# State loop of a two-layer network: whole uses of a PSUM bank, a piece cut in three, copies that alternate between two buffers, pieces handed out later

## Chip, cores and metric

One core of a Trainium2 chip runs the whole program as one launch. The metric is the device time of that launch in microseconds, median of several runs. The core's engines run their own instruction queues in order and wait for one another through semaphores: TensorE (PE in the profile, its weight loads PEld), VectorE (DVE), ScalarE (ACT), GpSimd (POOL) and SyncE (SP, which here only starts DMA transfers).

## The reference, cut to what matters

Two transformer-like layers on 64 sequences of 64 tokens with 256 features, all in float32. The first layer has a conditioned scan, an attention with 16 heads and a quantized feed-forward net. In the second, a recurrent net feeds a selective state-space block, and then come a mixture of experts with a shared expert and a second mixture. The change is in the state-space block and in the shared expert:

```python
xz = x @ W_in                       # 256 -> 2 x 512: xi and the gate z
xc = silu(causal_conv(xi) + b_conv) # four taps
delta_lr, B, C = split(xc @ W_xproj, [16, 32])
delta = softplus(delta_lr @ W_dt + b_dt)
dA  = exp(delta[..., None] * A)     # 512 channels x 16 states
dBx = delta[..., None] * B[:, :, None, :] * xc[..., None]
h   = dA_t * h + dBx_t              # along the 64 tokens
y   = sum_n(h * C_t) + D * x_t
out = (y * silu(z)) @ W_out

h = silu(x @ s_w1.T) * (x @ s_w3.T) # the shared expert, two of them side by side
shared = h @ s_w2.T
```

## The kernel before

Features lie on the 128 partitions and tokens along the free axis. Tokens are cut into eight chunks of 512 (eight whole sequences each). The function `mamba` runs the state-space block as one loop of 256 steps, 32 for each chunk. A step `j` of a chunk treats one state `n` (16 of them) of one pair of channel blocks `p` (two pairs of two blocks of 128). The first half of a chunk's steps has pair 0, the second half pair 1.

What one step does:

- `inputs` (L1046, two steps ahead, on POOL): hb = dx times the row of B, over 128 x 1024. The row of B is spread over the partitions by a DMA (Bn, L993, on SP), two states per transfer, in two buffers. hb has five buffers.
- `decay` (L1053, one step ahead, on ScalarE): dA = exp(delta * A), two activations of 128 x 504, into three PSUM banks that are used in turn.
- two scans (L1094, VectorE): h = dA * h + hb, each over 512 tokens.
- one product (L1096, VectorE): hb times cb. cb is the row of C spread over the partitions by a matmul (L998) into the one PSUM bank `cb`, one step ahead; the next such matmul waits until the product has read the bank.
- eight transposing matmuls (L1109, TensorE) that sum the products of a half's 16 states in the two banks `yp0` and `yp1`.

Everything else is handed out in pieces beside the steps. `turn` takes one piece at a time out of two streams:

- `urgent`: `finish` (L1006, L1008, L1009: transposing the sums back, adding D * xc, multiplying with the gate), after each half; and after a chunk's last step `project` (L1023, L1026: the output projection in two blocks of 256/2 rows, four matmuls each, added to x; a load of x, L1016, and a store, L1028, on SP).
- `pieces`: `gates` (L982, L985, L988: the matmuls of z, copies, SiLU) for a pair, and `head` of the next chunk: four blocks of convolution (L919 matmuls, L923 on ScalarE, three taps L926 on VectorE each), a SiLU (L930), the projection to delta, B and C (L934 to L947, with the store of B by L940), and for each pair delta and dx (L958 matmuls, L959 to L964 and L969 on ScalarE, then L967, L970, L971, L972 on POOL, or on VectorE for chunk 0).

A generator that yields `MID` is half-way through a use of the bank `mp`, the one bank that all pieces share. `turn` goes on with `pieces` after any `MID`, also one that came out of `urgent` (only `project` yields such a one). In each chunk 40 turns are spread evenly over the 32 steps: that is the number of pieces of a chunk. A loop in front of `inputs` takes extra turns if the delta and dx of a step that comes up aren't made.

A third stream, `others`, is the work of the mixture for the chunk before (`Mixture.beside`): its routing scores (L1499, L1505, L1511), from chunk 5 on the sending of rows (`send`: a load of `xr`, L1794, transposes L1802, copies L1803, eight indirect DMAs L1343 on POOL), and the shared expert (`shared`): matmuls L1820, four for each copy, into the one bank `mq`, copies L1824 (first factor) and L1827 (second factor, into the tile `up`, which POOL multiplies in by L1828), one SiLU L1831, matmuls L1836 and the scaled copy L1840 into `up`, stored by L1842. All these tiles have one buffer each.

The program is written with a layer that builds the dependencies and orders each engine's instructions at build time, by their place in the program and by its own cost estimates; the two scans and the product of the steps keep their written order. So a piece that is handed out elsewhere may move other instructions too.

ScalarE holds one set of function tables at a time. Exp, Ln and SiLU are in different sets here; the profile shows each change as ACT_TABLE_LOAD.

After the loop, `mixtures` runs the experts' tiles, with the shared expert of the last chunk and the sending of three further chunks between its first tiles.

Of the kernel before, what the change touches and what calls it, by code (L numbers as in the profile page):

```python
# [13 lines left out]
F32 = mybir.dt.float32  # L14
# [7 lines left out]
P = 128  # L22
B, L, D = 64, 64, 256
NT = B * L
CH = 512
NCH = NT // CH
KD = D // P
# [830 lines left out]
MID, END = "mid", "end"  # L858


def mamba(g, w, hs, beside):
# [3 lines left out]
    nc, tc = g.nc, g.tc  # L865
    NI, S, R = w.NI, w.S, w.R
# [3 lines left out]
    NB = 2  # L870
    PI = 2
    STEPS = NI // PI * S
    LEFT = 40
    BESIDE = 56
    BESIDE_LAST = 72
    hs2 = hs.rearrange("p k b t -> p k (b t)")
# [1 line left out]
    with (  # L878
# [17 lines left out]
        rows = 2 * 32 + S  # L896
# [12 lines left out]
        def head(c, v):  # L909

            tok = ts(c, CH)
            v.xc = p2.tile([P, NI, CH], F32, name="xc")
            v.delta, v.dx, v.sz, v.ready = [], [], [], 0
            v.dbc = p1.tile([W, CH], F32, name="dbc")
            v.parts = parts[c % 2]
            for i in range(NI):
                ps = one()
                for k in range(KD):
                    nc.tensor.matmul(ps, w.Win[:, k, ts(i, P)], hs2[:, k, tok], start=(k == 0), stop=(k == KD - 1))  # L919
                    if k == 0:  # L920
                        yield MID
                acc = v.xc[:, i, :]
                nc.scalar.activation(acc, ps, AF.Identity, bias=w.col[:, 0, i : i + 1], scale=w.taps[:, i, 3:4])  # L923
                for s in range(1, 4):
                    to = seq(acc)[:, :, s:]
                    nc.vector.scalar_tensor_tensor(  # L926
                        to, seq(ps)[:, :, : L - s], w.taps[:, i, 3 - s : 4 - s], to, ALU.mult, ALU.add
                    )
                yield
            nc.scalar.activation(v.xc, v.xc, AF.Silu)  # L930
            yield
            ps = one()
            for i in range(NI):
                nc.tensor.matmul(ps[:W, :], w.Wxp[:, i, :], v.xc[:, i, :], start=(i == 0), stop=(i == NI - 1))  # L934
                if i < NI - 1:
                    yield MID
            nc.scalar.copy(v.dbc, ps[:W, :])

            v.B = tc.dram_tile((S, CH), F32, name=f"B{c}")
            nc.sync.dma_start(v.B, v.dbc[R : R + S, :])  # L940


            r = slice(C0, W)
            nc.scalar.copy(v.parts[32 : 32 + S, :], ps[r, :])
            nc.vector.tensor_sub(ps[r, :], ps[r, :], v.parts[32 : 32 + S, :])
            nc.scalar.copy(v.parts[0:S, :], ps[r, :])
            nc.vector.tensor_sub(v.parts[64 : 64 + S, :], ps[r, :], v.parts[0:S, :])  # L947
            yield


            for i0 in range(0, NI, PI):
                z, u = (p3.tile([P, PI, CH], F32, name=n) for n in ("delta", "dx"))
                v.delta.append(z)
                v.dx.append(u)
                t2, t3 = (p1.tile([P, PI, CH], F32, name=n) for n in ("t2", "t3"))
                for i in range(PI):
                    ps = one()
                    nc.tensor.matmul(ps, w.Wdt[:, ts(i0 + i, P)], v.dbc[:R, :], start=True, stop=True)  # L958
                    nc.scalar.activation(z[:, i, :], ps, AF.Relu, bias=w.col[:, 1, i0 + i : i0 + i + 1])  # L959
                    nc.scalar.activation(u[:, i, :], ps, AF.Abs, bias=w.col[:, 1, i0 + i : i0 + i + 1])  # L960
                    yield
                nc.scalar.activation(u, u, AF.Exp, scale=-1.0)
                nc.scalar.activation(t2, u, AF.Identity, bias=unit[:, 0:1])
                nc.scalar.activation(t3, t2, AF.Identity, bias=unit[:, 1:2])  # L964
                yield
                e = nc.gpsimd if c else nc.vector
                e.tensor_sub(u, t3, u)  # L967
                yield
                nc.scalar.activation(t2, t2, AF.Ln)  # L969
                e.tensor_add(z, z, t2)  # L970
                e.tensor_sub(z, z, u)  # L971
                e.tensor_mul(u, z, v.xc[:, i0 : i0 + PI, :])  # L972
                v.ready += PI
                yield
# [94 lines left out]
        urgent, pieces, others = iter(()), iter(()), iter(())  # L1069
        mid = None  # L1070

        def turn():

            nonlocal mid
            got = next(pieces, None) if mid else next(urgent, END)
            if got is END:
                got = next(pieces, None)
            mid = got

        for s in range(LAST):  # L1080
            c, j = divmod(s, STEPS)
            p, n = divmod(j, S)
            now = vs[c]
            if j == 0:
                ahead = head(c + 1, vs[c + 1]) if c + 1 < NCH else iter(())
                pieces = chain(pieces, gates(c, now, 0), islice(ahead, 3 * NI + PI + 4), gates(c, now, PI), ahead)
                left = 0
            if n == 0:
                yp = [pp.tile([P, CH // P, P], F32, name=f"yp{i}") for i in range(PI)]
            hb, dA = hbs.pop(s), decays.pop(s)  # L1090

            for i in range(PI):
                h = hb[:, i, :]
                ins = nc.vector.tensor_tensor_scan(h, dA[i].rearrange("p b l -> p (b l)"), h, 0.0, ALU.mult, ALU.add)  # L1094
                tc.stamp_issue_order_token(ins.ins, "state")
            ins = nc.vector.tensor_tensor(hb, hb, cb.unsqueeze(1).to_broadcast([P, PI, CH]), ALU.mult)  # L1096
            tc.stamp_issue_order_token(ins.ins, "state")
            if s + AHEAD < LAST:
                ca, ja = divmod(s + AHEAD, STEPS)
                while vs[ca].ready <= ja // S * PI:  # L1100
                    turn()
                inputs(s + AHEAD)
            if s + 1 < LAST:
                decay(s + 1)
                cb = spread_c(vs[(s + 1) // STEPS], (s + 1) % S)

            for i in range(PI):
                for t in range(CH // P):
                    nc.tensor.matmul(  # L1109
                        yp[i][:, t, :],  # L1110
                        hb[:, i, ts(t, P)],
                        g.ident,
                        start=(n == 0 and t == 0),
                        stop=(n == S - 1 and t == CH // P - 1),
                        is_transpose=True,
                        skip_group_check=True,
                    )
            if n == S - 1:
                yT = [p1.tile([P, CH // P, P], F32, name=f"yT{i}") for i in range(PI)]
                for i in range(PI):  # L1120
                    nc.scalar.copy(yT[i], yp[i])
                urgent = chain(urgent, finish(c, now, p * PI, yT))
                if j == STEPS - 1:
                    urgent = chain(urgent, project(c, now))
            while left < (j + 1) * LEFT // STEPS:
                left += 1
                turn()
            most = BESIDE if c + 1 < NCH else BESIDE_LAST
            for _ in range((j + 1) * most // STEPS - j * most // STEPS):
                next(others, None)  # L1130
# [578 lines left out]
class Mixture:  # L1709
# [97 lines left out]
    def shared(self, c, x, work):  # L1807

        g, nc = self.g, self.g.nc
        NS = self.s1.shape[2] // P  # L1810
        UT = CH // 2
        for u in range(2):
            xu = x[:, :, ts(u, UT)]
            h = work.tile([P, NS, UT], F32, name="sh")
            for w in (self.s1, self.s3):
                for i in range(NS):
                    if i % 2 == 0:
                        ps = bank(g, (P, 2, UT))
                    for k in range(KD):
                        nc.tensor.matmul(ps[:, i % 2, :], w[:, k, ts(i, P)], xu[:, k, :], start=(k == 0), stop=(k == KD - 1))  # L1820
                    if i % 2:
                        to = h[:, i - 1 : i + 1, :]
                        if w is self.s1:
                            nc.scalar.copy(to, ps)  # L1824
                        else:
                            up = work.tile([P, 2, UT], F32, name="up")
                            nc.scalar.copy(up, ps)  # L1827
                            nc.gpsimd.tensor_mul(to, to, up)  # L1828
                    yield
                if w is self.s1:  # L1830
                    nc.scalar.activation(h, h, AF.Silu)  # L1831
                    yield
            ps = bank(g, (P, 2, D))
            for t in range(2):
                for i in range(NS):
                    nc.tensor.matmul(ps[:, t, :], h[:, i, ts(t, P)], self.s2[:, i, :], start=(i == 0), stop=(i == NS - 1))  # L1836
                    if i % 2 and (t, i) != (1, NS - 1):
                        yield
            rows = work.tile([P, 2, D], F32, name="up")
            nc.scalar.mul(rows, ps, 0.125)  # L1840
            to = self.made[c * CH + u * UT : c * CH + (u + 1) * UT, :]
            nc.sync.dma_start(to.rearrange("(t p) d -> p t d", p=P), rows)  # L1842
# [346 lines left out]
```

## Time and profile before

| | us |
|---|---|
| median of three runs (2806.24 to 2814.49) | 2806.84 |
| the profiled execution | 2807.03 |
| its span | 2804.6 |
| state loop, from the first scan to the last step | 698.5 to 1846 |
| what follows the loop | 1846 to 2804.6 |
| busy in the whole span: TensorE / VectorE / ScalarE / POOL | 2339.3 / 1770.7 / 1375.5 / 1340.5 |

Length of the eight chunks, from the first scan of one to the first scan of the next, read from the timeline of VectorE:

| chunk | 0 | 1 | 2 | 3 | 4 | 5 | 6 | 7 |
|---|---|---|---|---|---|---|---|---|
| us | 135.5 | 136.9 | 142.6 | 143.0 | 158.0 | 140.9 | 143.3 | 147 |

A line of the costliest groups reads: line, engine, operation, tile written and tiles read, shapes, count, then the group's busy time and the mean of one in ns, and last the engine's idle time ahead of it with what ended most of it. A line of waits reads: who waited, for whom, us in total, how often, and the longest. A timeline line has the start, the length, the engine and the instruction, and in brackets how long the engine had been idle and what ended that.

### The profile page before, as it was taken

To read this page: it belongs to the slowest core of one execution; us is meant where nothing else is said; L and a number is where in the kernel's file an instruction comes from. 1 tells how busy PE (TensorE), PEld (TensorE's weight loads), DVE (VectorE), ACT (ScalarE), POOL (GpSimd) and SP (SyncE) were. 2 spreads that over 40 slices of the span, in tenths; PEclk is the share of its full clock that TensorE was granted. 3 is DMA by queue.
4 is the path that set the end of the run, shared out by engine and by line. 5 is a ranking of instruction groups with operands and counts; after the bars stand their busy time and mean duration, and the time that the engine had idled before them with its cause. 6 is when DMAs were issued, how large, how long until landed. Compare 5 with 4: busy or idle time off the path is not lost.

```text
span 2804.6 us, 34388 instructions
## 1 busy us (share of the span) xinstructions
PE 2339.3 (83%) x11977; PEld 1674.0 (60%) x11996; DVE 1770.7 (63%) x2980; ACT 1375.5 (49%) x2289; POOL 1340.5 (48%) x1166
## 2 busy tenths in 40 slices
PE   3989967996568888887978888687786989999995
PEld 3634436773345555554655555566664768888884
DVE  0477748973999898888889797852353442322333
ACT  0567528885466757584757676533232222222220
POOL 0022345521696868685878787835555331111110
PEclk9979988997769999998999999899998999999997
DMA  9999820002112122221121222325685755555655
GB/s 224 372 358 347 276 70 1 1 1 90 68 68 83 65 74 70 72 72 57 65 92 67 83 81 75 106 70 178 212 287 194 278 216 206 214 192 197 227 192 189
DMA packets 180501, 406.03 MB, mean 145 GB/s; under 512 B 24785, under 2 KB 84434, under 8 KB 174946
## 3 DMA queue, kind: packets, MB, share of 16 engines
q1 hardware_dynamic: 166882, 366.80, 38.4%
q0 software_dynamic: 13440, 36.98, 3.4%
q8 instruction: 96, 1.57, 0.2%
q14 instruction: 83, 0.68, 0.1%
HBM read 280.76 MB, written 144.98 MB: 152 GB/s over the span
## 4 chain that ended last, share of the span: by engine, by line
PE 43%; DVE 21%; ACT 13%; issue 9%; POOL 5%; another core or an unknown queue 2%; DMA 1%; DVEq 0%; SPq 0%; ACTq 0%; POOLq 0%
DVE hb L1094 12%; PE ps L1684 11%; PE acc L1582 8%; PE out L450 4%; DVE hb L1096 3%; ACT dA L1053 2%; PE ps L1651 2%; PE yp L1109 2%; PE mq L1820 1%; DVE xc L926 1%; PE s L416 1%; PE acc L441 1%; ACT L1053 1%; PE mp L982 1%
## 5 line engine op out<-in xcount | busy, mean ns | idle before, releaser
L1046 POOL TENSOR_TENSOR hb<-dx,Bn 128x1024 f32<-128x1024 f32 x256 | 606.4, 2377 | 269.0 <-PE yp L1109 219.7
L1094 DVE TENSOR_TENSOR_SCAN hb<-dA,hb 128x512 f32<-128x512 f32 x512 | 602.1, 1210 | 63.2 <-ACT dA L1053 59.8
L1053 ACT ACTIVATE dA<-delta,negA 128x504 f32<-128x504 f32 x512 | 345.6, 685 | 303.5 <-DVE hb L1094 298.3
L1109 PEld LDWEIGHTS yp<-ident,hb 128*128 128x128 f32 x2048 | 264.4, 150 | 160.2 <-issue 121.2
L1096 DVE TENSOR_TENSOR hb<-hb,cb 128x1024 f32<-128x1024 f32 x256 | 312.4, 1220 | 66.3 <-PE cb L998 48.0
L1684 PE MATMUL ps<-gxT,w 128*128 128x256 f32 (+1 forms) x1600 | 324.5, 361 | 1.2 <-DVE gxT L1559 0.8
L1684 PEld LDWEIGHTS ps<-gxT,w 128*128 128x128 f32 x1600 | 276.3, 190 | 47.2 <-issue 12.4
L1820 PE MATMUL mq<-x,moe_s 128*128 128x256 f32 x896 | 244.5, 405 | 66.1 <-ACT up L1827 29.9
L1109 PE MATMUL yp<-ident,hb 128*128 128x128 f32 x2048 | 298.6, 290 | 0.0
L1358 POOL DMA_INDIRECT ffn_y<-gy,to x72 | 69.2, 962 | 432.3 <-ACT gy L1584 419.8
L1820 PEld LDWEIGHTS mq<-x,moe_s 128*128 128x128 f32 x896 | 166.6, 200 | 131.7 <-ACT sh L1824 42.5
L1688 DVE TENSOR_TENSOR gh<-gs,ps 128x256 f32<-128x256 f32 (+1 forms) x200 | 78.6, 394 | 213.5 <-ACT gs L1687 206.2
L1582 PE MATMUL acc<-w,gh 128*128 128x256 f32 (+1 forms) x864 | 190.0, 390 | 0.0
L1584 ACT ACTIVATE gy<-acc,wt 128x256 f32<-128x256 f32 x152 | 67.4, 474 | 246.8 <-PE acc L1582 227.5
L1687 ACT ACTIVATE gs<-ps 128x256 f32<-128x256 f32 (+1 forms) x200 | 72.4, 364 | 235.4 <-PE ps L1684 219.3
L998 PE MATMUL cb<-parts,pick 80*128 80x512 bf16 x256 | 104.5, 408 | 88.2 <-DVE hb L1096 83.9
L1582 PEld LDWEIGHTS acc<-w,gh 128*128 128x128 f32 (+1 forms) x864 | 146.8, 191 | 30.4 <-issue 13.2
L432 POOL TENSOR_TENSOR E<-E,z 128x1024 f32<-128x1024 f32 x32 | 61.6, 1925 | 194.5 <-DVE z L431 118.0
L1358 POOL DMA_INDIRECT moe_y<-gy,to x80 | 78.0, 975 | 110.2 <-ACT gy L1584 91.3
L1582 PE MATMUL acc<-w,rh 128*128 128x256 f32 x320 | 88.5, 419 | 45.6 <-ACT rh L1653 40.3
L1572 DVE TENSOR_REDUCE wt<-pick 128x2 f32<-128x4 f32 (+1 forms) x88 | 13.6, 156 | 174.7 <-ACT gy L1584 164.0
L450 PE MATMUL out<-oT,hs 128*128 128x512 f32 x256 | 117.8, 604 | 1.5 <-ACT oT L443 1.5
(470 smaller groups left out, 4457.1 us busy)
## 6 DMA issues: line engine op xcount, KB each, us to landing
w<-ffn_w SPq DMA_DIRECT2D x40, 2176.0 KB
Bn<-B SPq DMA_DIRECT2D x128, 512.0 KB
moe_x<-fill SPq DMA_DIRECT2D x130, 260.0 KB
ffn_x<-fill SPq DMA_DIRECT2D x129, 260.0 KB
w<-moe_w SPq DMA_DIRECT2D x48, 512.0 KB
ffn_w<-in_ffn_W_dram SPq DMA_DIRECT2D x16, 640.0 KB
gx<-moe_x SPq DMA_DIRECT2D x32, 260.0 KB
gx<-ffn_x SPq DMA_DIRECT2D x32, 260.0 KB
```

What stands on the lines that cost most here:

```text
L450: nc.tensor.matmul(ps, M[:, o, ts(k, P)], v.o[:, o], start=(o == 0), stop=(o == H // 2 - 1))
L998: nc.tensor.matmul(t, pick[:, n : n + 1].to_broadcast([rows, P]), v.parts, start=True, stop=True)
L1046: nc.gpsimd.tensor_mul(hb, vs[c].dx[p], Bn[:, n % NB, :].unsqueeze(1).to_broadcast([P, PI, CH]))
L1053: nc.scalar.activation(decays[s][i][:, :, 1:], seq(vs[c].delta[p][:, i, :])[:, :, 1:], AF.Exp, scale=A[:, p * PI + i, n : n + 1],)
L1094: ins = nc.vector.tensor_tensor_scan(h, dA[i].rearrange("p b l -> p (b l)"), h, 0.0, ALU.mult, ALU.add)
L1096: ins = nc.vector.tensor_tensor(hb, hb, cb.unsqueeze(1).to_broadcast([P, PI, CH]), ALU.mult)
L1109: nc.tensor.matmul(yp[i][:, t, :], hb[:, i, ts(t, P)], g.ident, start=(n == 0 and t == 0), stop=(n == S - 1 and t == CH // P - 1), is_tran ...
L1358: i = self.g.nc.gpsimd.indirect_dma_start(out=self.y, out_offset=bass.IndirectOffsetOnAxis(ap=to, axis=0), in_=y, in_offset=None)
L1582: nc.tensor.matmul(po[s], h, w, start=(i == 0), stop=(i == n - 1))
L1684: nc.tensor.matmul(ps[:, j, :], v.w12[:, k, ts(j * (full + 1) + i, P)], v.xT[:, k, :], start=(k == 0), stop=(k == KD - 1))
L1688: nc.vector.tensor_mul(v.h[:, i, : v.rows], s, ps[:, 1, :])
L1820: nc.tensor.matmul(ps[:, i % 2, :], w[:, k, ts(i, P)], xu[:, k, :], start=(k == 0), stop=(k == KD - 1))
```

## The change

- `turn` remembers the stream that yielded `MID` and goes on with that one until the use of the bank is over.
- Delta's last piece (Ln, L970, L971, L972) is cut in three: the Ln; L970; L971 and L972. A chunk then has 44 pieces instead of 40, and the point at which the gates of the second pair come in is moved by two, so that it stays behind delta's first half.
- In chunk 0 only 36 turns are handed out (`LAG` = 8); in the other chunks 44. So the last eight pieces of each chunk, delta's second half among them, run in the next chunk.
- In the shared expert the second factor's copies, and the scaled copy at the end, alternate between the tile `xr` (which `send` also uses) and `up`.

```diff
-    LEFT = 40
+    LEFT = 44
+    LAG = 8
...
+                e = nc.gpsimd if c else nc.vector
                 nc.scalar.activation(u, u, AF.Exp, scale=-1.0)
...
                 nc.scalar.activation(t2, t2, AF.Ln)
+                yield
                 e.tensor_add(z, z, t2)
+                yield
                 e.tensor_sub(z, z, u)
                 e.tensor_mul(u, z, v.xc[:, i0 : i0 + PI, :])
...
-            got = next(pieces, None) if mid else next(urgent, END)
-            if got is END:
-                got = next(pieces, None)
-            mid = got
+            if mid is None:
+                mid = urgent
+            got = next(mid, END)
+            if got is END and mid is urgent:
+                mid = pieces
+                got = next(mid, END)
+            if got is not MID:
+                mid = None
...
-                pieces = chain(pieces, gates(c, now, 0), islice(ahead, 3 * NI + PI + 4), gates(c, now, PI), ahead)
+                pieces = chain(pieces, gates(c, now, 0), islice(ahead, 3 * NI + PI + 6), gates(c, now, PI), ahead)
...
-            while left < (j + 1) * LEFT // STEPS:
+            while left < (j + 1) * (LEFT - (0 if c else LAG)) // STEPS:
...
+        def spare():
+
+            if next(names) == "up":
+                return work.tile([P, 2, UT], F32, name="up")
+            t = work.tile([P, KD, CH], F32, name="xr").rearrange("p k t -> p (k t)")
+            return t[:, : 2 * UT].rearrange("p (a t) -> p a t", a=2)
+
+        names = cycle(("xr", "up"))
...
-                            up = work.tile([P, 2, UT], F32, name="up")
+                            up = spare()
...
-            rows = work.tile([P, 2, D], F32, name="up")
+            rows = spare()
```

More of the change, by code (lines that the diff above doesn't have):

```diff
@@ L965, in head @@
                 yield
-                e = nc.gpsimd if c else nc.vector
                 e.tensor_sub(u, t3, u)
```

## The prediction

> **What bounds the kernel now.** I read the page first, then the loop alone (698 to 1846 us): its waits, then its timeline step by step, then the stretches of the eight chunks.
>
> ```profile
> span 2804.6 us, 34388 instructions
> ...
> L1094 DVE TENSOR_TENSOR_SCAN hb<-dA,hb 128x512 f32<-128x512 f32 x512 | 602.1, 1210 | 63.2 <-ACT dA L1053 59.8
> L1096 DVE TENSOR_TENSOR hb<-hb,cb 128x1024 f32<-128x1024 f32 x256 | 312.4, 1220 | 66.3 <-PE cb L998 48.0
> ```
>
> VectorE carries the loop: per step two scans and one product, and where nothing disturbs them the first scans of successive steps stand 3.57 us apart in the timeline. 256 steps x 3.57 = 914 of the loop's 1148 us. The rest is other VectorE work (taps L926, L1008, L1026, routing) and waits. The waits of VectorE in the loop:
>
> ```profile
> DVE hb L1094 <- ACT dA L1053: 59.8, 38, 7.6
> DVE hb L1096 <- PE cb L998: 48.0, 34, 4.9
> DVE hb L1094 <- POOL hb L1046: 3.1, 1, 3.1
> DVE mp L945 <- ACT parts L944: 2.3, 1, 2.3
> DVE xc L1008 <- PE mp L1006: 2.1, 2, 1.7
> ```
>
> Together 115 us: the change removes no VectorE work, so this is about all that it can win. The largest single kind of the cb wait (chunk 2, step 5):
>
> ```profile
> 992.19 0.67 DVE L1026 TENSOR_TENSOR x<-x,mp 128x512 f32<-128x512 f32 x1
> 992.31 0.69 ACT L1053 ACTIVATE dA<-delta,negA 128x504 f32<-128x504 f32 x1 [0.43 <-DVE hb L1094]
> 992.91 3.38 PE L982 MATMUL mp<-hs,Win 128*128 128x512 f32 x4 [2.20 <-DVE x L1026]
> 996.08 1.37 PE L1836 MATMUL mq<-moe_s,sh 128*128 128x256 f32 x4
> 996.32 0.59 ACT L985 COPY sz<-mp 128x512 f32<-128x512 f32 x1 [3.33 <-PE mp L982]
> 997.28 0.38 PE L998 MATMUL cb<-parts,pick 80*128 80x512 bf16 x1
> ...
> 997.70 1.22 DVE L1096 TENSOR_TENSOR hb<-hb,cb 128x1024 f32<-128x1024 f32 x1 [4.85 <-PE cb L998]
> ```
>
> A gate's matmuls (L982) stand between the halves of the output projection (L1023). They need the one bank mp, which L1026 frees late, and cb is queued behind them.
>
> **The change part by part.**
>
> *Whole uses of a bank.* Going through the steps' timelines, the waits of L1096 that lie at this place are 4.85 and 4.85 (chunks 2, 3), 3.16 and 3.16 (4, 5), 1.91+4.09 (6), 4.02+1.07 (7): 27.1 us. The instruction order of the built changed program has the eight L1023 of a chunk with no gate between them. In chunks 1 to 4 the second output block's matmuls stand one step after the first's, and L1026 stands ahead of the scans: no wait. In chunks 5 to 7, L1023 of the second block stands ahead of the next cb and waits for L1026, which stands behind two scans: 2.3 (two scans) + 0.67, then 1.0 (two L1023), 0.5 (two L1836), 0.38 (cb) end 4.9 us after the step starts, where the product wanted it at 3.1: 1.8 us x 3 = 5.4. Gain 27.1 - 5.4 = 21.7.
>
> *Later hand-out and two more pieces.* These move ScalarE's work, which is judged by how far ScalarE may run ahead. The first decay of a step can start when scan 2 of the step two before is done, the second when scan 1 of the step before is. Counting from step starts (3.57 apart; scan 1 ends at 1.25, both at 2.33; a decay takes 0.69 and the next starts 0.61 after it), 4.6 us of other work fit between two decays with no wait if ScalarE was idle before, and the backlog shrinks by 3.57/2 - 0.61 = 1.18 per gap. What a table change costs:
>
> ```profile
> 1107.95 0.68 ACT L1053 ACTIVATE dA<-delta,negA 128x504 f32<-128x504 f32 x1
> 1108.65 1.28 ACT L969 ACT_TABLE_LOAD   x1
> 1109.95 1.06 ACT L969 ACTIVATE t<-t 128x1024 f32<-128x1024 f32 x1
> 1110.91 0.57 ACT L1827 COPY up<-mq 128x512 f32<-128x512 f32 x1
> 1111.50 1.28 ACT L1053 ACT_TABLE_LOAD   x1
> ```
>
> Load to next start is 1.30, so a trip to Ln is 1.3+1.0+1.3 = 3.6, to Silu for L1831 4.4. The Trainium skill ("ScalarE: Activation LUTs", What ACT_TABLE_LOAD costs) has another 1.38 us of draining per switch. That speaks against this change, because in chunks 1 to 3 it parts L988 and L1831, which shared one trip: one trip more a chunk, 3 x 2.6 us by the row and 3 x 5.3 by the page, 8 us worse. I take the row, where no such gap is seen.
>
> Does the count fit the present kernel? End of chunk 2, by gap (other work): 1.0; 7.7 (L988, L1831); 1.15; 2.6; 1.05; 4.1. Backlogs over 4.6: 3.1, 1.4, 2.8 = 7.3; measured 3.0+0.47+0.59+0.35+2.36 = 6.8. Chunk 4: counted 9.4, measured 10.4.
>
> Same count on the new order. Chunks 1 to 3: step 24: 2.6, 2.6; step 25: 4.1 (Ln), 4.4 (L1831): waits 2.4 and 3.2. Step 30: 5.75 (L985, L988, L1827, L959, L960), 1.65: 1.2 and 0.5. Steps 11 and 12: L988, then L1824, L923, L1831 in one gap: 2.8. The Ln of the second half is now alone in step 2: none. Sum 10.0 each; before 5.9, 8.0, 8.0: a loss of 8. Chunk 4: 6.8 against 10.4. Chunks 5 and 6: 1.0 (Ln), 3.0+1.3 (joint trip, then L962, L963), 0.9 small: 6.2 against 9.1 and 10.1. Chunk 7: L1803 no longer waits for its scatter, because the eight L1343 stand together, right after the first rows: 1.9 against 6.3. Chunk 0: no change. All: 59.8 to 53, gain 7.
>
> *POOL and SP.* The second half of delta and dx now comes into being at steps 0 to 5 of its own chunk; the first decay and hb that read it belong to step 16, so some ten steps lie between, and without them it would cost one step for each that it is late. With delta's last piece in three, one or two 2.36 us products (L970 to L972) stand between two hb instead of three. The one POOL wait of 3.1 goes. All of POOL's work stays within its lead: hb may be made when yp five steps back is read. The store of B (L940), the load of x (L1016) and the store of x (L1028) go to SP some steps earlier or later; they take 0.3 to 0.4 us there, and SP has time (below).
>
> *Other places.* The product L945 comes a step later than L944: the 2.3 us goes; the L1008 in chunk 4 stand as elsewhere: 2.1 go. The remaining cb waits, 48.0 - 27.1 = 20.9, come from L1511 and L1820 groups ahead of cb. Their new places have more room (a group of four L1820 is 1.0 to 1.2 us), but I didn't find room everywhere: 13 left, gain 8.
>
> *Copies in two buffers.* ScalarE no longer waits for L1828 before a copy. In the loop that is 3 us of ScalarE idle time (all of the group less the part after the loop), hidden. After the loop four such waits sum to 11.3 us, beside TensorE's own work: I take 2 of it, between 0 and 8. The cost: the load of xr for `send` (L1794) waits on SP for a product on POOL, and queued behind it are Bn loads, which hb and the scan need. That is four loads in chunks 5 to 7. SP already stands 935 us in all before Bn loads, waiting for POOL (125 times, 7.5 us each), so a short wait is covered. Nothing to 3 us each; I take nothing.
>
> *TensorE's clock.*
>
> ```profile
> 698.00:834.00 136.00, 84.13 (x327) 53.64 (x328) 127.88 (x116) 82.77 (x109) 102.35 (x44) 0.69 0.18 63
> 834.00:971.00 137.00, 114.59 (x535) 75.05 (x535) 124.83 (x119) 93.89 (x128) 103.87 (x50) 0.96 0.23 79
> ```
>
> Columns: busy PE, weight loads, VectorE, ScalarE, POOL, granted clock, DMA share, GB/s. In chunk 0 the clock is 0.69 and eight transposes take 1.91 instead of 1.04. The skill ("TensorE: Matmul & The Clock Gate", Why this matters for your kernels) says that pauses over about 3 us put TensorE back to half rate, and the lag thins chunk 0's matmuls. At half rate throughout, a step's cb and transposes take 0.6 + 1.9 = 2.5 of 3.57 us: hidden. By the row 0; if the rule held in other chunks too, cb would be late by perhaps 1 us in five steps of each, 35 us in all. Chunks 1 to 7 keep their matmuls, so I take 0.
>
> *Sum.* 21.7 + 7 + 3.1 + 4.4 + 8 + 2 = 46.2 us off the profiled execution of 2807.03 us (span 2804.6, 2.4 around it), which is 0.2 above the median: 2761. What follows the loop (958 us, in which TensorE is busy for 850) starts earlier by as much.
>
> **Rivals.** (A) *Only the projection pays.* The ScalarE count is good to some 10%, but the gains of chunks 4 to 7 hang on waits for mq copies that I followed in part only. If ScalarE's sum stays level or worsens by the 8 of chunks 1 to 3, and other cb waits stay: 21.7 + 2 to 5 = about 24: 2783. For it: three chunks get worse by count.
> (B) *Slower: ScalarE and TensorE wait in turn.* At steps 12 and 26 of chunks 1 to 3, and 15 and 30 later, an L1820 group waits in TensorE's queue for a copy behind the 4.4 us trip of L1831, with cb behind it. I have cb's delay inside ScalarE's. If they add, a chunk loses up to 5 at each: 10 x 7 = 70, less 46: 2830. It decides from (46+8)/7 = 7.7 us a chunk. Against it: in the present kernel the same trips show only the decay's wait.
> (C) *No change:* the gains move into other waits; within 0.3% (8 us, about what these runs can tell).
> That the change doesn't do what it says is partly so: chunks 5 to 7 still pass a late L1026.
>
> **Chances.** Main 0.60 (2742 to 2778), A 0.22 (2778 to 2798), C 0.06, B 0.12. Faster 0.82, same 0.06, slower 0.12. The range takes in the unknowns: down to 2742 if the 13 us of cb waits and 6 of the tail go too, up to 2812 for A and most of C; about 0.18 is left out.
>
> **What would show it.** Right: L1096's wait for cb falls from 48 to some 18 us, with none over 3 at L1023; the decay's wait is near 53, with new waits at steps 12, 25 and 26 of chunks 1 to 3; no wait for L944; loop about 44 us shorter, the rest about 2. Wrong: a decay sum above 75, cb waits beside L1820 above 25, or a scan waiting for hb whose Bn was late.

## The result

The changed kernel takes 2775.08 us (median of four runs, 2770.22 to 2778.27) against 2810.19 for the kernel before (2806.24 to 2814.49). The ratio is 0.988, with an interval from 0.9858 to 0.9903. The forecast was 2761 us: the direction was right and the time lies in the range, but the gain is 35 us where the sum had 46.

The page of the changed kernel, the rows that answer to those of before:

```profile
span 2773.0 us, 34417 instructions
...
L1101 DVE TENSOR_TENSOR_SCAN hb<-dA,hb 128x512 f32<-128x512 f32 x512 | 601.5, 1207 | 56.3 <-ACT dA L1056 55.8
L1103 DVE TENSOR_TENSOR hb<-hb,cb 128x1024 f32<-128x1024 f32 x256 | 311.8, 1218 | 43.5 <-PE cb L1001 24.8
```

The scans and products last as long as before (602.1 and 312.4 us). What changed is the idle time ahead of them: the wait for cb fell from 48.0 to 24.8 us, the wait for the decay only from 59.8 to 55.8. VectorE's waits in the changed kernel's loop (who waits, for whom, us in total, times, longest):

```profile
DVE hb L1101 <- ACT dA L1056: 55.8, 36, 3.5
DVE hb L1103 <- PE cb L1001: 24.8, 16, 4.1
...
DVE rtags L1793 <- POOL big L1790: 1.8, 1, 1.8
DVE xc L1011 <- PE mp L1009: 1.7, 2, 0.9
DVE x L1029 <- PE mp L1026: 1.2, 1, 1.2
DVE up L1512 <- DMA shared_rows<-up: 1.0, 1, 1.0
```

In the same count of waits (without the 1.8 us for the first dx, which both kernels have) the loop has 116.9 us before and 87.7 after, 29.1 less. The loop itself, from the first scan to the end of the last step, is 1148.4 us before and 1121.9 after, 26.5 less. What follows the loop got 2.2 us shorter, and the loop began 2.8 us earlier, at 695.7 us; in a second profile of the changed kernel it began at 699.8 us, so that shift is chance.

The largest kind of cb wait that is left stands in chunks 5, 6 and 7 at step 4, 3.16 us each. The timeline of the changed kernel in chunk 5 (start, length, engine and instruction, idle time before it):

```profile
1420.07 0.66 DVE L1029 TENSOR_TENSOR x<-x,mp 128x512 f32<-128x512 f32 x1
...
1420.79 1.98 PE L1026 MATMUL mp<-xc,mWout 128*128 128x512 f32 x4 [2.46 <-DVE x L1029]
...
1422.61 1.03 PE L1852 MATMUL mq<-moe_s,sh 128*128 128x256 f32 x4
...
1423.47 0.38 PE L1001 MATMUL cb<-parts,pick 80*128 80x512 bf16 x1
...
1423.89 1.22 DVE L1103 TENSOR_TENSOR hb<-hb,cb 128x1024 f32<-128x1024 f32 x1 [3.16 <-PE cb L1001]
```

TensorE waits for the add that frees the bank, then runs two written matmuls of the second block and two of the shared expert, and only then cb. Each of these written f32 matmuls is recorded as two: the eight of a chunk's projection leave 16 records, and "x4" stands for two. The transposing ones (L1116, eight for each step) are recorded once.

### The profile page after: what moved, and what is told of

Same layout as the page of the kernel before. It is cut to its first block, busy times and chain, and to the rows that moved or that the text cites. A ratio compares the mean times of both kernels' runs of the same rounds, so it can differ in the third digit from the quotient of the medians.

```text
span 2773.0 us, 34417 instructions
## 1 busy us (share of the span) xinstructions
PE 2326.7 (84%) x11977; PEld 1670.5 (60%) x11996; DVE 1773.6 (64%) x2980; ACT 1383.4 (50%) x2298; POOL 1340.5 (48%) x1166
## 4 chain that ended last, share of the span: by engine, by line
PE 43%; DVE 23%; ACT 11%; issue 9%; POOL 4%; another core or an unknown queue 2%; DMA 1%; SPq 0%; DVEq 0%; ACTq 0%; POOLq 0%
DVE hb L1101 13%; PE ps L1691 11%; PE acc L1589 8%; PE out L450 4%; DVE hb L1103 4%; PE ps L1658 2%; ACT dA L1056 2%; PE yp L1116 2%; PE mq L1836 1%; PE acc L441 1%; PE s L416 1%; DVE xc L927 1%; PE ps L1699 1%; PE mp L1026 1%
## 5 line engine op out<-in xcount | busy, mean ns | idle before, releaser
L1101 DVE TENSOR_TENSOR_SCAN hb<-dA,hb 128x512 f32<-128x512 f32 x512 | 601.5, 1207 | 56.3 <-ACT dA L1056 55.8
L1116 PEld LDWEIGHTS yp<-ident,hb 128*128 128x128 f32 x2048 | 263.7, 150 | 176.7 <-issue 145.2
L1103 DVE TENSOR_TENSOR hb<-hb,cb 128x1024 f32<-128x1024 f32 x256 | 311.8, 1218 | 43.5 <-PE cb L1001 24.8
L1116 PE MATMUL yp<-ident,hb 128*128 128x128 f32 x2048 | 297.8, 289 | 0.0
L1836 PE MATMUL mq<-x,moe_s 128*128 128x256 f32 x896 | 243.6, 408 | 40.7 <-ACT sh L1840 22.6
L1836 PEld LDWEIGHTS mq<-x,moe_s 128*128 128x128 f32 x896 | 170.6, 202 | 107.5 <-ACT sh L1840 37.4
```

The source lines that it names most:

```text
L1116: nc.tensor.matmul(yp[i][:, t, :], hb[:, i, ts(t, P)], g.ident, start=(n == 0 and t == 0), stop=(n == S - 1 and t == CH // P - 1), is_tran ...
```

## The experiments

They ran on two chips. On the first the kernel before takes 2755.7 to 2756.2 us, and on the second, which had the four runs from "When does the gate come back?" on, 2753.6, not 2810 as in the first comparison. The loop lasts the same there (a second profile of the changed kernel has 1119.9 us), but what follows it is some 50 us shorter; why is not known. So times are compared as ratios to the kernel before on the same chip, and loops in microseconds. The changed kernel itself was measured again on the first of the two chips alone, and the loop of the kernel before is that of its one profile, in the first comparison.

> The changed kernel itself, beside the others of this set. Both theories: ratio to the kernel before 0.988 as at first (about -33 us), last step of the loop at 1814 us.

Measured: 2725.19 us, ratio 0.9888 (0.9868 to 0.9909), as expected. The last step begins at 1816.0 us instead of 1814.0, because the loop began later.

All kernels, in order of time. "Gate between" says whether the instruction order has a gate's matmuls between the halves of the output projection; decay, cb and other are VectorE's waits in the loop in us, summed step by step from one profile of each kernel.

| kernel | gate between | ratio | interval | loop | decay | cb | other |
|---|---|---|---|---|---|---|---|
| cut alone | yes | 1.0089 | 1.0071 to 1.0108 | 1169.2 | 63.8 | 43.3 | 26.0 |
| old turn, 4 late | yes | 1.0078 | 1.0065 to 1.0092 | 1171.5 | 66.0 | 46.4 | 22.9 |
| turn alone | no | 1.0002 | 0.9989 to 1.0015 | 1151.7 | 66.4 | 36.3 | 18.2 |
| before | yes | 1 | | 1148.4 | 59.8 | 48.0 | 9.1 |
| late hand-out alone | no | 0.9979 | 0.9969 to 0.9988 | 1144.1 | 58.2 | 39.4 | 12.3 |
| old turn, 6 late | no | 0.9978 | 0.9969 to 0.9987 | 1143.5 | 65.4 | 31.6 | 13.5 |
| extra turn between blocks | no | 0.9964 | 0.995 to 0.9977 | 1141.1 | 65.5 | 18.3 | 21.0 |
| uncut | no | 0.9955 | 0.9938 to 0.9972 | 1140.4 | 49.0 | 24.1 | 33.2 |
| one buffer | no | 0.9902 | 0.9884 to 0.992 | 1122.9 | 56.3 | 25.5 | 7.5 |
| changed, again | no | 0.9888 | 0.9868 to 0.9909 | 1119.9 | 56.3 | 24.4 | 5.9 |
| no late hand-out | no | 0.9881 | 0.9863 to 0.99 | 1117.1 | 60.7 | 25.4 | 3.1 |
| old turn | no | 0.9827 | 0.9808 to 0.9845 | 1108.5 | 49.5 | 25.8 | 4.9 |
| changed, SiLU left out | no | 0.9821 | 0.9807 to 0.9834 | 1100.8 | 29.1 | 26.5 | 12.3 |

But for the first two (0.11% apart), the loops stand in the order of the times: what differs is mainly the loop. What follows it lies between 899.6 and 907.1 us on these chips.

**Each part undone.** My theory (P) was that the new turn rule carries most of the gain. First it was put back:

```diff
-            if mid is None:
-                mid = urgent
-            got = next(mid, END)
...
+            got = next(pieces, None) if mid else next(urgent, END)
+            if got is END:
+                got = next(pieces, None)
+            mid = got
```

> The changed kernel with the old rule of turn alone (a MID of the projection hands the next turn to the gates). Theory P (whole uses of the bank carry most of the gain): the waits of the product for cb at the projection come back, 27 us where the changed kernel has 9.5, so about 18 us slower than the changed kernel, near 2793 us, sum of cb waits 40 or more. Rival S (the spacing of ScalarE's and POOL's work carries it, the planner finds a good order for TensorE anyway): within 5 us of the changed kernel, 2775 to 2780.

Measured: 2706.31 us, ratio 0.9827. The kernel didn't lose 18 us, it gained about 17 more. Theory P falls, and S, which allowed 5 us, is missed too. The waits of this kernel:

```profile
DVE hb L1097 <- ACT dA L1056: 49.5, 23, 5.8
DVE hb L1099 <- PE cb L1001: 25.8, 29, 3.1
```

cb waits no longer than in the changed kernel, although `turn` again goes over to `pieces` after a `MID` from `project`. In the order of TensorE no gate stands between the halves here either: at that place the pieces in line are the late ones of the chunk before, delta's second half, and not the gates. So the late hand-out keeps the gate out as well.

The decay waits are 6.7 us fewer than in the changed kernel's profile on this chip. ScalarE of the changed kernel in chunk 2, steps 24 to 26:

```profile
1075.80 1.28 ACT L970 ACT_TABLE_LOAD   x1
1077.10 1.06 ACT L970 ACTIVATE t<-t 128x1024 f32<-128x1024 f32 x1
...
1078.64 1.28 ACT L1056 ACT_TABLE_LOAD   x1
1079.94 0.69 ACT L1056 ACTIVATE dA<-delta,negA 128x504 f32<-128x504 f32 x1
1080.64 1.28 ACT L1847 ACT_TABLE_LOAD   x1
1081.94 1.91 ACT L1847 ACTIVATE sh<-sh 128x2048 f32<-128x2048 f32 x1
1083.87 1.28 ACT L1056 ACT_TABLE_LOAD   x1
```

And with the old turn rule at the same place (L1843 is the shared expert's SiLU there):

```profile
1076.50 1.28 ACT L970 ACT_TABLE_LOAD   x1
1077.80 1.06 ACT L970 ACTIVATE t<-t 128x1024 f32<-128x1024 f32 x1
1078.88 1.28 ACT L1843 ACT_TABLE_LOAD   x1
1080.17 1.91 ACT L1843 ACTIVATE sh<-sh 128x2048 f32<-128x2048 f32 x1
1082.10 1.28 ACT L1056 ACT_TABLE_LOAD   x1
```

Ln and SiLU go one after the other with one way back to Exp; in the changed kernel one decay stands between them and costs a load more. Here the old rule's waits are 5.2 us (step 26), the new rule's 0.87, 3.55 and 2.74 (steps 25 and 26). Over chunks 1 to 3 the decay waits are 22.3 us against 34.5; in chunks 4 to 7 they are 27.3 against 21.4. All waits together explain 6.4 of the 11.4 us by which the loop is shorter; VectorE's own busy time in it is 3.9 us less, and what follows the loop 6.4 us less, for reasons that weren't traced.

**One buffer for all copies:**

```diff
-        names = cycle(("xr", "up"))
+        names = cycle(("up",))
```

> The changed kernel with all second-factor copies of the shared expert in one tile (up), as before. Theory P: copies in two buffers hide nothing but some us after the loop: 0 to 5 us slower than the changed kernel, 2775 to 2780. Rival B (two buffers let the matmul groups of mq follow one another, and that frees cb): 10 us or more slower, 2785 and up, with more waiting for mq copies on POOL.

Measured: 2728.27 us, ratio 0.9902 against 0.9888, with intervals that overlap; the loop is 1122.9 us against 1119.9 and 1121.9 in the two profiles of the changed kernel, and what follows it 907.1 against 906.6 on the same chip. The two buffers do nothing that can be seen.

**No late hand-out:**

```diff
-    LAG = 8
+    LAG = 0
```

> The changed kernel with all 44 turns handed out in chunk 0 too, so that delta's second half is made in the chunk before, as before the change. Theory P: the lag only moves ScalarE's load from one chunk's end to the next one's start; the wait for decays stays within 6 us of 55.8, time within 6 us of the changed kernel. Rival S: the lag is what loosens the end of a chunk; 10 us or more slower, 2785 and up, all in the wait for decays at steps 28 to 31 and 0.

Measured: 2720.63 us, ratio 0.9881: the same as the changed kernel. Where the new turn rule keeps the gate out, the late hand-out isn't needed.

**The piece uncut**, with 40 turns:

```diff
-    LEFT = 44
+    LEFT = 40
...
                 nc.scalar.activation(t2, t2, AF.Ln)
-                yield
                 e.tensor_add(z, z, t2)
-                yield
...
-islice(ahead, 3 * NI + PI + 6)
+islice(ahead, 3 * NI + PI + 4)
```

> The changed kernel with delta's last piece in one again (40 turns, 32 of them in chunk 0; the lag of eight stays). Theory P: scans wait for hb by some 3 us more, time 0 to 5 us above the changed kernel. Rival S: the cut is what keeps POOL's products apart; 10 us or more slower.

Measured: 2745.27 us, ratio 0.9955: 18 us of the gain are lost. The waits of this kernel's loop:

```profile
DVE hb L1099 <- ACT dA L1054: 49.0, 27, 6.6
DVE hb L1101 <- PE cb L999: 24.1, 29, 3.6
DVE up L1510 <- DMA shared_rows<-up: 11.3, 3, 4.2
DVE xc L927 <- ACT xc L924: 7.9, 3, 2.8
```

Decay and cb wait no longer than in the changed kernel. The time is S's, but not for its reason: scans wait for POOL only 2.6 us in all. What grew is everything else: the routing's `up` waits for the store of the shared expert's rows from the same tile, once in each of chunks 5 to 7, and the taps wait for ScalarE.

**Each part alone.** The new turn rule on the kernel before:

```diff
-            got = next(pieces, None) if mid else next(urgent, END)
...
+            got = next(mid, END)
...
+            if got is not MID:
+                mid = None
```

> The kernel before with the new turn rule alone. In its instruction order the eight L1026-type matmuls of a chunk stand together with no gate between. Theory P (whole uses are worth about 20 us wherever they are reached): cb waits of the loop from 48 to about 28, time -22 us (ratio 0.992). Rival Q (the gain needs the cut piece as well, since without it whole uses with the late hand-out gave only -6.5 us in the loop): within 8 us of before (ratio 0.997 to 1.003).

Measured: 2754.88 us, ratio 1.0002. cb falls by 11.7 us and not by 20, and decay (+6.6) and the rest (+9.1) take more than that back, L1026 alone 10.3. Theory P falls here too; the time is what Q expected.

The cut and 44 turns on the kernel before:

```diff
-    LEFT = 40
+    LEFT = 44
...
                 nc.scalar.activation(t2, t2, AF.Ln)
+                yield
                 e.tensor_add(z, z, t2)
+                yield
...
```

> The kernel before with delta's last piece in three and 44 turns alone. Its order still has a gate between the halves of the output projection. Theory P: cb waits stay at 45 to 50, and only what the cut removes by itself goes: 2.8 us ahead of the loop, 2.3 (L945 behind L944), 3.1 (POOL): -8 us (ratio 0.997). Rival Q (the cut is the main part: with all other edits in place its removal cost 23 us of the loop): -18 to -25 us (ratio about 0.992).

Measured: 2778.9 us, ratio 1.0089, slower by 24 us: outside both theories. Its longest wait, 10.26 us in chunk 2, comes from this stretch of ScalarE:

```profile
1101.83 0.69 ACT L1055 ACTIVATE dA<-delta,negA 128x504 f32<-128x504 f32 x1
...
1106.31 1.28 ACT L1833 ACT_TABLE_LOAD   x1
1107.60 1.91 ACT L1833 ACTIVATE sh<-sh 128x2048 f32<-128x2048 f32 x1
...
1112.08 1.28 ACT L1055 ACT_TABLE_LOAD   x1
1113.38 1.89 ACT L1055 ACTIVATE dA<-delta,negA 128x504 f32<-128x504 f32 x3
```

11.55 us lie between the starts of two decays: with the spread of 44 turns the SiLU falls between delta's Exp and what follows it, and all of that stands ahead of the next decay. In the sum this is not the loss, however. Against the kernel before, decay has grown by 4.0 us only and cb fallen by 4.7, while the other waits rose from 9.1 to 26.0:

```profile
DVE xc L1010 <- PE mp L1008: 12.6, 10, 2.6
DVE mp L945 <- ACT parts L944: 8.4, 4, 4.0
```

L1010 (adding D * xc) waits for its transposes and L945 for ScalarE: the pieces now land at steps where what they need isn't done. The other 4.6 of the loop's 20.8 us are not in the waits; VectorE's busy time rose by 4.4.

The late hand-out on the kernel before:

```diff
+    LAG = 8
...
-            while left < (j + 1) * LEFT // STEPS:
+            while left < (j + 1) * (LEFT - (0 if c else LAG)) // STEPS:
```

> The kernel before with the late hand-out alone (eight pieces later, 40 turns, old turn rule, piece uncut, one buffer). Its order has no gate between the halves of the projection, because delta's pieces stand there in place of the gates. Theory P: as the turn rule alone, -22 us (ratio 0.992), cb waits about 28. Rival Q: within 8 us of before, with the gain in cb given back in other waits of VectorE.

Measured: 2748.29 us, ratio 0.9979. cb falls by 8.6 and not by 20; of it 3.2 go to the other waits, and decay falls by 1.6. The time is Q's.

Alone the parts give 0, +24 and -6 us; together -31. They don't add up. With the runs above, all eight combinations of the three parts are measured (the pairs have the two copy buffers as well, which by the run with one buffer do little). Turn rule and late hand-out without the cut reach 0.9955, the cut with the turn rule 0.9881, the cut with the late hand-out 0.9827. So the cut costs where the gate stands between and gains where it is out; the gain belongs to the cut together with either way of keeping the gate out, and both ways together are no better than one.

**When does the gate come back?** With the old turn rule, a hand-out four pieces late has the gate between the halves, one six or eight pieces late hasn't. New theory (R): the gain stands or falls with that gate.

```diff
-    LAG = 8
+    LAG = 4    # the second run: 6
```

> The changed kernel with the old turn rule (as in the run that reached ratio 0.983) and a hand-out four pieces late instead of eight. Its instruction order has a gate's matmuls between the halves of the output projection again; cut, 44 turns and two buffers stay. Theory R (the gain stands or falls with whether a gate gets between the halves; turn rule and late hand-out are two ways to keep it out): the gain is lost, as with the cut alone: ratio 1.00 to 1.01, cb waits above 40. Rival S (each piece of delay brings its share, or times scatter with the placement): about halfway between 0.983 and 1.009, 0.996.

Measured with four: 2774.1 us, ratio 1.0078, as R said: from 0.9827 across to slower than before. TensorE of this kernel at step 5 of chunk 2:

```profile
991.36 1.88 PE L1026 MATMUL mp<-xc,mWout 128*128 128x512 f32 x4
...
996.67 2.60 PE L985 MATMUL mp<-hs,Win 128*128 128x512 f32 x4 [2.57 <-DVE x L1029]
999.07 1.91 PE L1848 MATMUL mq<-moe_s,sh 128*128 128x256 f32 x4
1000.77 0.63 PE L1001 MATMUL cb<-parts,pick 80*128 80x512 bf16 x1
```

The product then waits 4.83 us: it is the place, and the wait, of the kernel before (4.85). In both, part of it is TensorE at half rate (last section).

> As the one before with a hand-out six pieces late. Its order has no gate between the halves in chunks 1 to 7. Theory R: ratio 0.980 to 0.988, cb waits about 26. Rival S: between the one with four and the one with eight, about 0.990.

Measured with six: 2747.7 us, ratio 0.9978. cb is 31.6 us, nearer to R's 26 than to the 46 with the gate; but decay is 65.4 where eight gave 49.5, and two scans wait 3.1 us each for POOL. R's time is missed by 1%, S's by 0.8%. So R is half right: in these runs cb waits 43 to 48 us with the gate between and 18 to 39 us without it; but how much of that is kept depends on what the same shift does to ScalarE.

**One more turn between the two blocks**, for the three waits of 3.16:

```diff
-    LEFT = 44
+    LEFT = 45
...
                     if i % 2 and i < NI - 1:
                         yield MID
+                if k == 0:
+                    yield
```

> The changed kernel with one more turn between the two blocks of the output projection (45 turns), so that the matmuls of the second block come a turn behind those of the first. In chunks 5 to 7 the order no longer has them together ahead of one cb. If the three cb waits of 3.16 us behind L1026 are a matter of that order alone: they go, -9.5 us against the changed kernel (ratio to before 0.985). Rival: the shift of all later pieces by one turn moves ScalarE's table trips and other waits by as much, and the result is anywhere within 10 us of the changed kernel, with the 3.16s gone but others in their place.

Measured: 2742.98 us, ratio 0.9964. The 3.16s are gone, cb is 18.3, the least of all kernels. Yet by the ratios the kernel is about 21 us slower than the changed one, more than either expectation allowed. Two rows show where most of it went:

```profile
DVE hb L1103 <- ACT dA L1058: 65.5, 35, 4.5
...
DVE x L1029 <- PE mp L1026: 8.9, 4, 2.7
```

Decay took 9 us more, and L1029 8 more: in chunks 1 to 4 it now stands at a step where its matmuls aren't done.

**Without the shared expert's SiLU.** The identity stands for it, so that this function is left out of the computation:

```diff
-                    nc.scalar.activation(h, h, AF.Silu)
+                    nc.scalar.activation(h, h, AF.Identity)
```

> The changed kernel with the shared expert's SiLU (L1847) replaced by the identity of the same shape: it leaves out that SiLU and with it its table trips, 2.6 us each by the rows of the trace, where no other SiLU shares them. Theory U (ScalarE may have 4.6 us of other work between two decays): the decay waits of chunks 1 to 4 at steps 12, 25 and 26 fall by 20 us or so, from 56 to about 35; time -22 us against the changed kernel (ratio to before 0.980). Rival V (decays are not what ends last there; TensorE's cb is late soon after): decay waits fall, cb waits rise by as much, time within 8 us of the changed kernel.

Measured: 2705.74 us, ratio 0.9821, by the ratios about 18 us faster than the changed kernel. Its waits:

```profile
DVE hb L1101 <- ACT dA L1056: 29.1, 26, 2.4
DVE hb L1103 <- PE cb L1001: 26.5, 21, 3.2
DVE hb L1101 <- POOL delta L972: 4.3, 2, 2.1
```

The instruction is as long as before (1.90 us); only its table loads are gone, 77 in the loop instead of 101. The decay waits fell by 27 us, more than U's 21, and cb rose by only 2: V falls. In chunk 2 the decay waits at step 12 went from 2.7 to 0.2, and those of steps 25 and 26 from 7.2 to 3.3. Some 8 us of the gain went to other waits, 4.3 of them to POOL's making of delta. So the decays do set the pace there, and the SiLU's table loads are a large part of what makes them late.

## Why the prediction was right or wrong

*What bounds the loop* was right: VectorE with its waits. The loop's waits were to fall by 44 us and fell by 29.1. That the sum came within 11 us of the result is in part luck, because no part does alone what its term says.

*Whole uses of a bank, 21.7 us.* The waits at this place fell from 27.1 to 9.5, 17.6 less; all of cb fell by 23.2 where 29.7 were forecast. 12.9 of the 17.6 come from chunks 2 to 4, where the second block now stands a step later. In chunk 5 the wait is 3.16 us with the gate in that place and 3.16 with the projection's own second block. As a cause the step failed: the new turn rule alone gives nothing (1.0002), and the kernel is faster with the old one (0.9827). What the step missed is that the late hand-out puts delta's pieces where the gate stood, so either part keeps the gate out; and that the new rule, on top of that, parts Ln and SiLU trips (the load of their table and the way back to Exp) which the old one joins.

*The three late L1026.* Chunks and mechanism were right, the size was not: 1.8 us was forecast and 3.16 measured, 4.1 us over three chunks. I had two L1023 at 1.0 and two L1836 at 0.5, which is what two records take. Two written ones leave four and take 1.98 and 1.03.

*ScalarE, 59.8 to 53.* Measured 55.8. The count of 4.6 us between two decays gave 10.0 for each of chunks 1 to 3 and found 10.4, 12.5 and 11.6; 6.8 and 8.3 in chunk 4; 6.2 and 5.0 or 6.1 in chunks 5 and 6; 1.9 and 2.0 in chunk 7. It also named the steps: 12, 25, 26, 30. The row for a table load was the right price: the next activation starts 1.29 to 1.30 us after the load. The further draining of 1.38 us that the Trainium skill states ("ScalarE: Activation LUTs", What ACT_TABLE_LOAD costs) isn't in these traces: in the fences above the next activation starts 0.01 to 0.02 us after the end of a load.

*The cut* had no term of its own: I counted 3.1 (POOL) and 2.3 (L945). Both waits went, POOL's to 0.2. But the cut is worth 18 us in the full change and costs 24 us alone. Here the step that failed is the method: a sum of parts, each against the kernel before. The cut also changes the spread of the turns from 40 to 44, so every piece lands on another step.

*Other cb waits, 8; clock, 0.* The other cb waits fell by 5.6. One that is left, in chunk 4, is 4.05 us with TensorE at half rate, which I had put at nothing. The clock was already in what I counted: by comparison with chunk 4, of the two waits of 4.85 us before, 1.69 each are half rate and not the gate (below).

*Small waits.* L1793, L1029 and L1512 are new with 4.0 us together, and L1011 still waits 1.7 us, in chunk 7, where I had taken off all 2.1.

*Copies, 2 after the loop.* The part after the loop got 2.2 us shorter in the first pair of profiles, but with one buffer it is only 0.6 us longer on the same chip, so that this was the copies isn't shown. ScalarE's waits for POOL's product after the loop did go (10.9 us with one buffer, none with two); they were hidden.

The shortfall of 15.1 us in the waits is thus: cb 6.4 (24.8 for 18.4), decay 2.8, new small waits 4.0, L1011 1.7, in all 14.9.

*Rivals.* B, the slower case, didn't come: no cb wait stands behind the decay's at step 12. A's 2783 is 8 us above the result, nearer than the 2761 of the sum, 14 below it; but its reason, that the projection pays by itself, isn't what the runs show. Of the signs of being right, the decay's sum, its steps and the end of the wait for L944 came true; "none over 3 at L1023" and "loop about 44 us shorter" didn't.

The step that failed is thus the sum itself, with the projection's 21.7 us as a gain of the turn rule and the cut without a term. What stays open: which of the moved pieces makes the cut a loss alone and a gain with the gate out. The runs show the waits that differ, not one cause, and no version was run that moves one piece and nothing else.

The old turn rule with the other three parts is the fastest version that computes everything: 2706.31 us, and its interval (0.9808 to 0.9845) lies below that of the changed kernel (0.9868 to 0.9909).

## What to carry to other kernels

When small pieces of work are handed out beside a loop that has deadlines on several engines, an edit acts through the step at which each piece lands: build each part alone and together, because here parts of 0, +24 and -6 us made -31. Look first in the instruction order for a foreign use of a shared bank between two halves (cb waits of 43 to 48 us with it, 18 to 39 without), then for table changes on ScalarE that could share a trip; removing a wait that is plain to see (three of 3.16) can cost more than it brings. Before pricing a matmul from the trace, count how many records one written matmul leaves.

## What the runs showed of the hardware

TensorE fell to half rate without a long pause. In the changed kernel's chunk 4 (stretch, its length, busy time of PE, granted clock, DMA share, GB/s):

```profile
1348.00:1352.00 4.00, 4.00 (x21) 1.00 0.38 141
1352.00:1356.00 4.00, 2.35 (x7) 0.87 0.16 48
1356.00:1360.00 4.00, 4.00 (x13) 0.50 0.46 149
1360.00:1364.00 4.00, 4.00 (x8) 0.50 0.00 0
```

The timeline of the same stretch:

```profile
1354.01 0.38 PE L1001 MATMUL cb<-parts,pick 80*128 80x512 bf16 x1 [1.31 <-DVE hb L1103]
1354.73 1.86 PE L959 MATMUL mp<-dbc,Wdt 16*128 16x512 f32 x2 [0.34 <-DVE parts L948]
...
1362.13 2.08 PE L1836 MATMUL mq<-x,moe_s 128*128 128x256 f32 x4
```

Pauses of 1.31 and 0.34 us came before it; the four records of L1836 then took 2.08 us, and the product waited 4.05 us. In the second profile of the same kernel the same two pauses were followed by a shorter slow stretch, 0.62 over four microseconds; there the same four records took 1.13 us, and that wait was 1.14 us.

The kernel before has such stretches too. At the gate between the halves TensorE had paused for 2.20 us in chunks 2 and 4 alike. In chunk 2 the gate's matmuls (992.91 in the prediction's timeline) took 3.38 us and the product waited 4.85; in chunk 4 they took 1.98 and the product waited 3.16:

```profile
1278.51 1.98 PE L982 MATMUL mp<-hs,Win 128*128 128x512 f32 x4 [2.20 <-DVE x L1026]
```

The granted clock of the two stretches, in the same columns as above:

```profile
994.00:996.00 2.00, 2.00 (x3) 0.50 0.01 2
...
1278.00:1280.00 2.00, 1.49 (x4) 1.00 0.71 242
```

The Trainium skill ("TensorE: Matmul & The Clock Gate", Why this matters for your kernels) speaks of pauses of over about 3 us; here shorter ones went before the half rate, after the same 2.20 us it came once and once not, and it ended at another time in each execution. What starts it wasn't tested.
